# A two-layer graph transformer: raw rows for layer 2's first chunks, batch-norm moments taken block by block, and other places for the table blocks

## The chip, the cores and the metric

The kernel runs on one core of a Trainium2 chip. The metric is the device time of one execution in microseconds. The kernel before takes 2332.54 us (median of three runs, 2331.6 to 2333.5).

## The reference

N = 6250 nodes with 128 features, E = 106250 edges sorted by destination (random pairs in both directions and one loop per node). Every edge has 64 given features and 32 made from a time difference; the two together are its `edge_attr`. Both layers are a transformer convolution with two heads of 64:

```
q, k, v = h@Wq+bq, h@Wk+bk, h@Wv+bv              # by node, 2 heads
e       = edge_attr @ We                          # by edge
alpha   = (q[dst] * (k[src] + e)).sum(c) / 8      # by edge and head
a       = softmax of alpha over the edges of one dst
out     = segment_sum((v[src] + e) * a, dst) + h@Ws + bs
```

and the whole is

```
edge_attr = [cos((node_vec[src] - edge_weight) * time_w + time_b), edge_attr_64]
h = conv1(x)
h = relu((h - mean(h)) / sqrt(var(h) + 1e-5) * bn_g + bn_b)     # over all nodes, by feature
y = layernorm(x + conv2(h))
```

What matters here is the line in the middle: mean and variance are taken over all 6250 nodes, so no row of layer 2's input is known in its final form before the last node of layer 1 is done. Everything is float32.

## The kernel before, in words

**Chunks.** The sorted edge list is cut into NC = 107 chunks of at most CE = 1024 edges (T = 8 tiles of 128) that belong to at most NN = 64 destination nodes. The function `conv(c, extra)` runs one layer as a software pipeline over these chunks. The loop is `for k in range(-AHEAD, NC + 3)` with AHEAD = 4, and one round of it does, in this order, for different chunks:

- `fetch(k + 4)` (L713 to 738): SP loads the chunk's edge features into the tile `ff`, a slice of the table into `ftab`, and in layer 2 also the encoded times (`fz`), the turned edge features (`fxT`) and 64 rows for the residual (`fr`);
- `gather(k + 4)` (L743): GpSimd issues eight indirect DMAs that fetch the source nodes' rows into `ff`, from `xv_d` in layer 1 and from `h_d` in layer 2;
- `score(k)` (L809, L810), `lowest(k)` (L815), `weigh(k)` (L822): scores of all edges against 64 nodes x 2 heads on TensorE, the minimum on VectorE, the exponential on ScalarE;
- `turn_weights(k - 1)` (L832, L833): the weights are transposed;
- `divide(k - 2)`, `finish_turn(k - 2)`, `finish(k - 2)` (L844 to L901): the sums are normalised and multiplied by the value weights; in layer 1 the 64 new rows are written as columns of the tile `hT` by an SP DMA (L870, `fhT<-fres`), in layer 2 they go to the layer norm and to the output;
- `turn_in(k + 1)` (L792, L793): the gathered rows are transposed on TensorE and copied by ScalarE to `fft`;
- `encode(k + 2)` or later (L760 to L774, layer 1): the time encoding; from chunk SINGLE = 24 on, two chunks share one sine on ScalarE, before that each has its own;
- `pull(extra, 1)`: one piece of other work, see below;
- `gather_sums(k - 1)` (L839): the weighted sums, eight matmuls.

The whole loop stands under a manual schedule: each engine's instructions stand in the order in which they are written. The tile `ff` has six buffers, so the gather of chunk k + 4 writes where chunk k - 2 was.

**Tables.** A score needs, for each destination node, four (layer 2) or five (layer 1) numbers per feature. They are made in 13 blocks of 512 nodes by `tables` (L622 to L637): one 128x512 matmul per piece (`fpg`, L627), an eviction by ScalarE (L629, L631) or VectorE (L633) into `fo`, and a store to `tab_d` from ScalarE's queue. `tables` is a generator and yields after each piece; `conv` draws pieces from it through `extra`. In layer 1, six pieces are pulled at the very start of the loop (k = -4), and then one in each round from k = -4 on. In layer 2, blocks 0 and 1 with their residual (L1030 to L1033) are made before the loop, and the rest one piece per round from k = -4 on.

**Between the layers** (L975 to L1014): ScalarE and VectorE sum `hT` (L982, L983), ScalarE sums the squares over all 6250 columns (L988), a few small operations give `scale` and `shift`; then 13 times: ReLU with scale and shift on ScalarE (L1003), four transposes on TensorE (L1006), a copy by VectorE (L1008) and a store of 512 rows to `h_d` by SP (L1011, L1014). Layer 2's first gather waits for the last of these stores, since it can address any row.

Of the kernel before, what the change touches and what calls it, by code (L numbers as in the profile page):

```python
# [621 lines left out]
def tables(nc, pl, c, fT, b0, work, bank):  # L622

    o = work.tile([P, GE, H, 3 - c], F32, name="fo", tag="fo")
    for i, (a, b) in enumerate(pl.mats[c]):
        pg = bank()
        nc.tensor.matmul(pg, a, fT, start=True, stop=True)  # L627
        if i == 2 * H:
            nc.scalar.activation(o[:, :, :, 2], pg[:, :, None].to_broadcast([P, GE, H]), AF.Identity, bias=b)  # L629
        elif i < H:  # L630
            nc.scalar.activation(o[:, :, i, 0], pg, AF.Identity, bias=b)  # L631
        else:
            nc.vector.scalar_tensor_tensor(  # L633
                o[:, :, i - H, 1].rearrange("p (b n) -> p b n", n=P), pg.rearrange("p (b n) -> p b n", n=P), b,
                pl.code[:, None, :].to_broadcast([P, GE // P, P]), op0=OP.add, op1=OP.add)
        if i == len(pl.mats[c]) - 1:
            nc.scalar.dma_start(pl.tab_d[c][:, b0 * GE:(b0 + 1) * GE], o)  # L637
        yield
# [22 lines left out]
def ordered(ctx: ExitStack, tc: tile.TileContext, pl, x, dst, edge_attr_64, conv2, bn_g, bn_b, out):  # L661
# [11 lines left out]
    h_d = dram.tile([N, D], F32, name="h_d")  # L673
    res_d = dram.tile([NP, D], F32, name="res_d")
# [17 lines left out]
    SINGLE = 24  # L692

    def conv(c, extra):
# [45 lines left out]
        def gather(k):  # L740
            f = ch[k].f
            for t in range(T):
                nc.gpsimd.indirect_dma_start(  # L743
                    out=f[:, t, (1 if c else 0):1 + D], out_offset=None, in_=h_d if c else pl.xv_d,
                    in_offset=bass.IndirectOffsetOnAxis(ap=pl.srcs[:, t, k:k + 1], axis=0))
# [37 lines left out]
        def turn_in(k, u):  # L783

            s = ch[k]
            if u == 0:
                s.ft = work.tile([P, CE], F32, name="fft")
                if c == 0:
                    s.et = work.tile([EC, CE], F32, name="fet")
            px = p_tr.tile([P, GE], F32, name="fpx", tag="tr")  # L790
            for t in range(4):
                nc.tensor.transpose(px[:, t * P:(t + 1) * P], s.f[:, u * 4 + t, 1:1 + D], ident)  # L792
            nc.scalar.copy(s.ft[:, u * GE:(u + 1) * GE], px)  # L793
            if c:
                return
            pe = p_tr.tile([P, GE], F32, name="fpe", tag="tr")
            for t in range(4):
                nc.tensor.transpose(pe[:EC, t * P:(t + 1) * P], s.f[:, u * 4 + t, 1 + D:], ident)
            nc.scalar.copy(s.et[:, u * GE:(u + 1) * GE], pe[:EC])  # L799
            if u:  # L800
                nc.sync.dma_start(et_d[k], s.et)
# [39 lines left out]
        def divide(k):  # L841
# [5 lines left out]
            nc.vector.tensor_scalar(s.a, s.pa, inv, None, op0=OP.mult)  # L847

# [62 lines left out]
        with cs, tc.manual_schedule():  # L911
            for k in range(-AHEAD, NC + 3):
# [6 lines left out]
                if k == -AHEAD and c == 0:  # L919
                    pull(extra, 6)  # L920
# [24 lines left out]
                pull(extra, 1)  # L945
# [4 lines left out]
                if c and on(k):  # L950
                    nc.vector.tensor_copy(ch[k].f[:, :, 1 + D:1 + D + TD], ch[k].z)
                for _ in range(min(len(done), 2 if k > NC - 12 else 1)):
                    store(*done.pop(0))
                if on(k - 1):
                    gather_sums(k - 1)
            for _ in extra:
                pass
# [6 lines left out]
    with tc.tile_pool(name="fpw", bufs=2) as pw:  # L964
        with tc.tile_pool(name="ftp", bufs=3, space=bass.MemoryType.PSUM) as mp, tc.manual_schedule():
            turn_features(nc, pl, mp, N)
        def rest():
            for b0 in range(1, NT):
                yield from tables(nc, pl, 0, xT[:, b0 * GE:(b0 + 1) * GE], b0, pw, lambda: pl.bank())
                if b0 == 2:  # L970
                    yield from load_others(nc, pl, const, conv2, bn_g, bn_b)
            yield from matrices(nc, pl, 1, const, lambda: pl.bank()[:, :P])

        conv(0, rest())
    nc.gpsimd.memset(hT[:, N:], 0.0)  # L975


    with tc.tile_pool(name="fbn1", bufs=1) as one, tc.tile_pool(name="fbnw", bufs=2) as pw:
        neg = one.tile([P, 2], F32, name="fmu")
        half = N // 2  # L980
        scr = pl.xT
        nc.vector.tensor_reduce(neg[:, 0:1], hT[:, :half], AX.X, OP.add)  # L982
        nc.scalar.activation(scr[:, half:N], hT[:, half:N], AF.Copy, accum_out=neg[:, 1:])  # L983
        mu = one.tile([P, 1], F32, name="fmu1")
        nc.vector.tensor_add(mu, neg[:, 0:1], neg[:, 1:])
        nc.vector.tensor_scalar(mu, mu, -1.0 / N, None, op0=OP.mult)
        var = one.tile([P, 1], F32, name="fbvar")
        nc.scalar.activation(scr[:, :N], hT[:, :N], AF.Square, bias=mu, accum_out=var)  # L988
        nc.vector.tensor_scalar(var, var, 1.0 / N, EPS, op0=OP.mult, op1=OP.add)
        nc.scalar.activation(var, var, AF.Sqrt)  # L990
        scale = one.tile([P, 1], F32, name="fscale")
        nc.vector.reciprocal(scale, var)
        nc.vector.tensor_mul(scale, scale, pl.bng)
        shift = one.tile([P, 1], F32, name="fshift")
        nc.vector.tensor_mul(shift, scale, mu)
        nc.vector.tensor_add(shift, shift, pl.bnb)
        NB = -(-N // P)
        with tc.tile_pool(name="fbnh", bufs=4) as hp, \
                tc.tile_pool(name="fbnp", bufs=2, space=bass.MemoryType.PSUM) as pps:
            for b0 in range(0, NB, 4):  # L1000
                n = min(4, NB - b0)
                cs_ = slice(b0 * P, b0 * P + GE)
                nc.scalar.activation(hT[:, cs_], hT[:, cs_], AF.Relu, bias=shift, scale=scale)  # L1003
                pt = pps.tile([P, 4, P], F32, name="fpt")
                for i in range(n):
                    nc.tensor.transpose(pt[:, i], hT[:, (b0 + i) * P:(b0 + i + 1) * P], ident)  # L1006
                hr = hp.tile([P, 4, P], F32, name="fhr")
                nc.vector.tensor_copy(hr[:, :n], pt[:, :n])  # L1008
                full = min(n, (N - b0 * P) // P)
                if full:  # L1010
                    nc.sync.dma_start(h_d[b0 * P:(b0 + full) * P, :].rearrange("(b p) d -> p b d", p=P), hr[:, :full])  # L1011
                if full < n:
                    left = N - (b0 + full) * P
                    nc.sync.dma_start(h_d[(b0 + full) * P:N, :], hr[:left, full])  # L1014
# [27 lines left out]
        with tc.tile_pool(name="fpp2", bufs=1, space=bass.MemoryType.PSUM) as pp:  # L1042
            pl.bank = lambda: pp.tile([P, GE], F32, name="fpg")
            for b0 in range(2):
                for _ in block(b0):
                    pass

        def rest():
            for b0 in range(2, NT):
                yield from block(b0)  # L1050

        conv(1, rest())
# [4 lines left out]
def tile_gnn_resnorm(ctx: ExitStack, tc: tile.TileContext, x, src, dst, edge_attr_64, edge_weight, node_vec,  # L1057
# [13 lines left out]
    with tc.tile_pool(name="plan", bufs=1) as pl, tc.tile_pool(name="planw", bufs=2) as mw, \  # L1071
# [7 lines left out]
        got.hT = keep.tile([P, NP], F32, name="fhT")  # L1079
        got.rest = keep.tile([P, 1 + D], F32, name="fxrest")  # L1080
# [27 lines left out]
        ones = pl.tile([P, P], F32, name="pones")  # L1108
# [157 lines left out]
```

## Time and profile before

| what | value |
|---|---|
| time, median of three runs | 2332.54 us |
| the profiled execution | 2840.8 us, span 2838.6 us |
| mean granted TensorE clock in the profile | 0.941 |
| busy: TensorE / VectorE / ScalarE / GpSimd | 84% / 44% / 44% / 58% |
| first layer 1 chunk turned on TensorE | 105.2 us |
| last TensorE work of layer 1 | 1447.2 us |
| first gather of layer 2 | 1480.2 us |
| last gather | 2777.8 us |

The profiled execution is longer than the shown runs by 508 us, so times in the profile are not parts of the 2332 us; a difference between two profiles is not the difference of two runs. The page's fifth part lists groups of instructions: line, engine, operation, output<-input, shape, count | busy us, mean ns | idle time of the engine just before them and what ended it. "issue" there is time in which the engine waited for nothing that the profile shows. In timelines a line is: start us, duration us, engine, line, operation, tiles, count, and in brackets the idle time before it. Some matmuls appear as two records ("x2").

### The profile page before, as it was taken

How to read it: one execution, taken by the hardware profiler on the slowest of the kernel's cores; microseconds unless marked ns; L12 is line 12 of the kernel's file. 1: busy time of each engine (PE TensorE's matmuls, PEld its weight loads, DVE VectorE, ACT ScalarE, POOL GpSimd, SP SyncE). 2: the span in 40 equal slices, each digit the busy share in tenths (PEclk: the TensorE clock that was granted, in tenths of full speed). 3: DMA queues.
4: the chain of work that ended last, by engine and by line, in shares of the span. 5: the costliest groups of instructions: out<-in, count | busy, mean ns of one | idle time of the engine just before them, and what ended most of it. 6: DMA issues, size and time to landing. Idle time of an engine off the chain costs nothing.

```text
span 2838.6 us, 39250 instructions
## 1 busy us (share of the span) xinstructions
PE 2380.1 (84%) x11637; PEld 1759.9 (62%) x11637; DVE 1246.3 (44%) x3735; ACT 1236.5 (44%) x1950; POOL 1637.7 (58%) x1733
## 2 busy tenths in 40 slices
PE   5589988888988888888965989988998888888887
PEld 3366766666776776666742666656666665666665
DVE  3446665555665566565621333333333222222223
ACT  2356664455554455544541333333433333333334
POOL 4356665655665666666415666666666666666661
PEclk7799999999999999999976999999999999999998
DMA  6345554555554445454425555655555454444541
GB/s 198 116 117 155 157 151 144 146 144 166 157 155 127 124 135 137 134 136 136 124 75 165 154 151 155 170 147 156 156 152 151 133 138 127 133 128 131 136 127 46
DMA packets 428354, 396.58 MB, mean 140 GB/s; under 512 B 282064, under 2 KB 371940, under 8 KB 424804
## 3 DMA queue, kind: packets, MB, share of 16 engines
q1 hardware_dynamic: 354406, 238.66, 30.3%
q0 software_dynamic: 55168, 114.12, 15.7%
q10 hardware_dynamic: 18558, 41.20, 3.9%
q8 instruction: 95, 1.56, 0.2%
q14 instruction: 127, 1.04, 0.1%
HBM read 279.72 MB, written 110.59 MB: 138 GB/s over the span
## 4 chain that ended last, share of the span: by engine, by line
PE 34%; issue 6%; another core or an unknown queue 3%; DVE 3%; DMA 2%; POOL 2%; ACT 1%; SPq 1%; DVEq 0%; ACTq 0%; POOLq 0%
PE fpa L839 11%; PE fps L809 6%; PE fps L810 5%; PE fppt L832 4%; PE fpx L792 3%; POOL ff L743 2%; PE fpo L875 1%; PE fpg L627 1%; DMA fr<-res_d 1%; PE fpo L853 1%; DMA ff<-h_d,fsrcs 1%; PE fpo L876 1%; DVE fa L847 1%; PE fpo L854 0%
## 5 line engine op out<-in xcount | busy, mean ns | idle before, releaser
L743 POOL DMA_INDIRECT ff<-xv_d,fsrcs x856 | 822.3, 961 | 568.3 <-issue 224.4
L743 POOL DMA_INDIRECT ff<-h_d,fsrcs x856 | 810.9, 947 | 517.9 <-issue 249.9
L839 PE MATMUL fpa<-ff,fpt 128*128 128x225 f32 x3424 | 714.6, 362 | 0.8 <-issue 0.8
L839 PEld LDWEIGHTS fpa<-ff,fpt 128*128 128x128 f32 x3424 | 645.9, 194 | 14.6 <-issue 0.9
L809 PE MATMUL fps<-fft,ftab 128*128 128x512 f32 x856 | 464.7, 622 | 74.2 <-issue 33.0
L793 ACT COPY fft<-fpx 128x512 f32<-128x512 f32 x428 | 250.2, 585 | 545.7 <-PE fpx L792 202.3
L832 PEld LDWEIGHTS fppt<-fident,fs 128*128 128x128 f32 x1712 | 208.6, 144 | 201.8 <-issue 194.9
L832 PE MATMUL fppt<-fident,fs 128*128 128x128 f32 x1712 | 253.8, 279 | 79.0 <-issue 77.0
L833 ACT COPY fpt<-fppt 128x512 f32<-128x512 f32 x428 | 227.6, 581 | 117.8 <-PE fppt L832 50.0
L822 ACT ACTIVATE fs<-fps,fm 128x1024 f32<-128x1024 f32 x214 | 238.7, 1115 | 66.1 <-issue 27.6
L815 DVE TENSOR_REDUCE flow<-fps 128x1 f32<-128x1024 f32 x214 | 260.0, 1215 | 12.5 <-PE fps L810 12.5
L792 PE MATMUL fpx<-fident,ff 128*128 128x128 f32 x1712 | 254.1, 284 | 12.1 <-DVE fbits L726 12.1
L891 ACT ACTIVATE fsq<-fy 64x128 f32<-64x128 f32 x107 | 33.1, 310 | 503.7 <-DVE fy L889 286.4
L887 DVE SCALAR_TENSOR_TENSOR fres<-fpo,fr 64x128 f32<-64x128 f32 x107 | 30.2, 282 | 501.5 <-PE fppt L832 211.0
L810 PE MATMUL fps<-fxT,ftab 112*128 112x512 f32 x428 | 231.3, 618 | 7.3 <-issue 6.4
L809 PEld LDWEIGHTS fps<-fft,ftab 128*128 128x128 f32 x856 | 171.7, 230 | 104.1 <-issue 56.1
L810 PE MATMUL fps<-fet,ftab 112*128 112x512 f32 x428 | 224.3, 605 | 0.8 <-issue 0.8
L792 PEld LDWEIGHTS fpx<-fident,ff 128*128 128x128 f32 x1712 | 209.8, 147 | 17.1 <-DVE fbits L726 13.7
L799 ACT COPY fet<-fpe 112x512 f32<-112x512 f32 x214 | 126.3, 590 | 198.1 <-PE fppt L832 56.0
L853 PEld LDWEIGHTS fpo<-fident,fa 128*128 128x128 f32 x214 | 30.5, 142 | 286.8 <-issue 184.9
L856 DVE COPY fat<-fpo 128x256 f32<-128x256 f32 x214 | 90.9, 425 | 247.9 <-PE fpo L854 102.5
L853 PE MATMUL fpo<-fident,fa 128*128 128x128 f32 x214 | 64.0, 299 | 157.1 <-DVE fa L847 95.3
(198 smaller groups left out, 2540.7 us busy)
## 6 DMA issues: line engine op xcount, KB each, us to landing
ff<-in_edge_attr SPq DMA_DIRECT2D x214, 256.0 KB
et_d<-fet SPq DMA_DIRECT2D x107, 448.0 KB
fxT<-et_d SPq DMA_DIRECT2D x107, 448.0 KB
ftab<-tab_d SPq DMA_DIRECT2D x107, 192.0 KB
tab_d<-fo ACTq DMA_DIRECT2D x13, 1536.0 KB
ff<-xv_d,fsrcs POOLq DMA_INDIRECT x856
enc_d<-fzs SPq DMA_DIRECT2D x107, 128.0 KB
ff<-h_d,fsrcs POOLq DMA_INDIRECT x856
```

The lines of the kernel that those rows point to most:

```text
L743: nc.gpsimd.indirect_dma_start(out=f[:, t, (1 if c else 0):1 + D], out_offset=None, in_=h_d if c else pl.xv_d, in_offset=bass.IndirectOffs ...
L792: nc.tensor.transpose(px[:, t * P:(t + 1) * P], s.f[:, u * 4 + t, 1:1 + D], ident)
L793: nc.scalar.copy(s.ft[:, u * GE:(u + 1) * GE], px)
L799: nc.scalar.copy(s.et[:, u * GE:(u + 1) * GE], pe[:EC])
L809: nc.tensor.matmul(s.ps[:, w], s.tab[:, :, 0], s.ft[:, w], start=True, stop=False)
L810: nc.tensor.matmul(s.ps[:, w], s.tab[:EC, :, 1], s.et[:, w], start=False, stop=True)
L815: nc.vector.tensor_reduce(low, s.ps, AX.X, OP.min)
L822: nc.scalar.activation(s.s, s.ps, AF.Exp, bias=s.bias, scale=-1.0)
L832: nc.tensor.transpose(pp[:, t * P:(t + 1) * P], s.s[:, at:at + P], ident)
L833: nc.scalar.copy(s.pt[:, u * GE:(u + 1) * GE], pp)
L839: nc.tensor.matmul(s.pa, s.pt[:, t * P:(t + 1) * P], s.f[:, t, 1:1 + D + EW], start=t == 0, stop=t == T - 1)
L853: nc.tensor.transpose(s.po[:, 0], s.a[:, :D], ident)
```

## The change

Five edits. (1) Layer 1's rows are passed on while layer 1 runs: `pass_rows` takes a block of 512 columns of `hT` once all chunks that can write to it are finished, transposes it, stores it unnormalised to `h_d`, and takes its moments with one `bn_stats`; after the loop, one `bn_aggr` joins the 13 moments. (2) Chunks 0 to 2 of layer 2 (RAW = 3) gather from this raw `h_d`. Their rows are normalised when needed: in `turn_in` by ScalarE, whose copy becomes a ReLU with scale and shift (features are partitions there), and in `normalise` by three VectorE operations for the sums. (3) All later chunks gather from a new tensor `hn_d`, which `first_blocks` writes at round k = -4 of layer 2: ReLU of the blocks, transposes, copies, and stores from ScalarE's queue instead of SP's. (4) Table blocks move: no piece is pulled before round 0; two per round are pulled in rounds 0 to 3 and after round 80; two empty steps follow each block; in layer 2 only block 0 is made ahead, through three PSUM banks instead of one. `fo` has one buffer instead of two. (5) SINGLE is 16 instead of 24. The diff has nothing else on the sine or its buffers.

```diff
-    o = work.tile([P, GE, H, 3 - c], F32, name="fo", tag="fo")
+    o = work.tile([P, GE, H, 3 - c], F32, name="fo", tag="fo", bufs=1)
...
-    SINGLE = 24
+    SINGLE = 16
+    RAW = 3
...
-                    out=f[:, t, (1 if c else 0):1 + D], out_offset=None, in_=h_d if c else pl.xv_d,
+                    out=f[:, t, (1 if c else 0):1 + D], out_offset=None, in_=(h_d if k < RAW else hn_d) if c else pl.xv_d,
...
-            nc.scalar.copy(s.ft[:, u * GE:(u + 1) * GE], px)
+            if c and k < RAW:
+                nc.scalar.activation(s.ft[:, u * GE:(u + 1) * GE], px, AF.Relu, bias=pl.shift, scale=pl.scale)
+            else:
+                nc.scalar.copy(s.ft[:, u * GE:(u + 1) * GE], px)
...
+        def normalise(k):
+            rows = ch[k].f[:, :, 1:1 + D]
+            for i, op in enumerate((OP.mult, OP.add)):
+                nc.vector.tensor_tensor(rows, rows, pl.spread[:, None, i].to_broadcast([P, T, D]), op)
+            nc.vector.tensor_scalar(rows, rows, 0.0, None, op0=OP.max)
...
-                if k == -AHEAD and c == 0:
-                    pull(extra, 6)
+                if k == -AHEAD and c:
+                    first_blocks()
...
-                pull(extra, 1)
+                if k >= 0:
+                    at_round[0] = k
+                    pull(extra, 2 if k < 4 or k > 80 else 1)
...
                 if c and on(k):
+                    if k < RAW:
+                        normalise(k)
...
+        def pass_rows(b0):
+            r0 = b0 * GE
+            n = min(GE, N - r0)
+            rows = turned_rows(b0)
+            nc.vector.bn_stats(stats[:, b0], hT[:, r0:r0 + n])
+            yield
+            put_rows(nc.sync, h_d, b0, rows)
+            yield
+        def turned_rows(b0):
+            r0 = b0 * GE
+            n = -(-min(GE, N - r0) // P)
+            pt = pl.bank().rearrange("p (b d) -> p b d", d=P)
+            for i in range(n):
+                nc.tensor.transpose(pt[:, i], hT[:, r0 + i * P:r0 + (i + 1) * P], ident)
+            rows = pw.tile([P, GE // P, P], F32, name="fhr", bufs=3)
+            nc.vector.tensor_copy(rows[:, :n], pt[:, :n])
+            return rows
...
         def rest():
+            others = load_others(nc, pl, const, conv2, bn_g, bn_b)
             for b0 in range(1, NT):
                 yield from tables(nc, pl, 0, xT[:, b0 * GE:(b0 + 1) * GE], b0, pw, lambda: pl.bank())
-                if b0 == 2:
-                    yield from load_others(nc, pl, const, conv2, bn_g, bn_b)
+                for _ in range(2):
+                    next(others, None)
+                    yield
             yield from matrices(nc, pl, 1, const, lambda: pl.bank()[:, :P])
+            for b0 in range(-(-N // GE)):
+                while at_round[0] < 3 + max(k for k in range(NC) if first(k)[0] < (b0 + 1) * GE):
+                    yield
+                yield from pass_rows(b0)
...
-        nc.vector.tensor_reduce(neg[:, 0:1], hT[:, :half], AX.X, OP.add)
-        nc.scalar.activation(scr[:, half:N], hT[:, half:N], AF.Copy, accum_out=neg[:, 1:])
...
-        nc.scalar.activation(scr[:, :N], hT[:, :N], AF.Square, bias=mu, accum_out=var)
...
+        nc.vector.bn_aggr(moments, stats)
...
-            for b0 in range(0, NB, 4):
-                n = min(4, NB - b0)
...
-                nc.scalar.activation(hT[:, cs_], hT[:, cs_], AF.Relu, bias=shift, scale=scale)
...
-                    nc.sync.dma_start(h_d[b0 * P:(b0 + full) * P, :].rearrange("(b p) d -> p b d", p=P), hr[:, :full])
...
+        def first_blocks():
+            for b0 in range(1, NT):
+                relu(b0)
+            for b0 in range(-(-N // GE)):
+                put_rows(nc.scalar, hn_d, b0, turned_rows(b0))
-        with tc.tile_pool(name="fpp2", bufs=1, space=bass.MemoryType.PSUM) as pp:
+        with tc.tile_pool(name="fpp2", bufs=3, space=bass.MemoryType.PSUM) as pp, tc.manual_schedule():
             pl.bank = lambda: pp.tile([P, GE], F32, name="fpg")
-            for b0 in range(2):
-                for _ in block(b0):
-                    pass
+            relu(0)
+            for _ in block(0):
+                pass
...
+            for i, col in enumerate((scale, shift)):
+                nc.vector.tensor_scalar(diag[:, i], ident, col, None, op0=OP.mult)
+                nc.tensor.matmul(pb[:, i], pl.ones, diag[:, i], start=True, stop=True)
+            nc.vector.tensor_copy(spread, pb)
         def rest():
-            for b0 in range(2, NT):
+            for b0 in range(1, NT):
                 yield from block(b0)
-        conv(1, rest())
+                yield
+                yield
+        conv(1, rest(), first_blocks)
```

`put_rows(eng, to, b0, rows)` is the store of one block of rows, as at L1011 and L1014, from the given engine's queue.

## The prediction

> **What bounds the kernel now.** I read the page's busy table first, then the chain of waits in the middle of a layer, then the engines' timelines around the two places where TensorE stands still: the fill of layer 1 and the turn from layer 1 to layer 2. The page:
>
> ```profile
> span 2838.6 us, 39250 instructions
> PE 2380.1 (84%) x11637; PEld 1759.9 (62%) x11637; DVE 1246.3 (44%) x3735; ACT 1236.5 (44%) x1950; POOL 1637.7 (58%) x1733
> L743 POOL DMA_INDIRECT ff<-h_d,fsrcs x856 | 810.9, 947 | 517.9 <-issue 249.9
> ```
>
> TensorE is the busiest engine; GpSimd looks half idle but its 856 gathers per layer each end in a fixed gap. The chain shows an undisturbed chunk of layer 1, when no gather runs any more (columns: start us, us, what):
>
> ```profile
> 1403.01 0.92 PE fps L809 x2
> 1403.94 0.86 PE fps L810 x2
> 1405.02 0.44 PE fpx L792 x4
> ...
> 1407.21 3.04 PE fpa L839 x16
> ...
> 1412.85 0.92 PE fps L809 x2
> ```
>
> From score to score 1403.01 to 1412.85 is 9.84 us of TensorE at full clock with nothing between. In layer 2 the same chain has fpa starts at 1932.46 and 1942.60: 10.14 us with one table piece (fpg, 0.87 us) in it, so 9.27 without. GpSimd in a run of gathers:
>
> ```profile
> 1481.46 0.95 POOL L743 DMA_INDIRECT ff<-h_d,fsrcs  x1 [0.30 <-issue]
> 1482.71 0.94 POOL L743 DMA_INDIRECT ff<-h_d,fsrcs  x1 [0.30 <-issue]
> ```
>
> One gather every 1.25 us, 8 per chunk: 10.0 us. So both engines need about 10 us per chunk, and they overlap. What overlaps with nothing is the fill and the turn. The turn on TensorE and in the chain:
>
> ```profile
> 1446.77 0.39 PE L864 MATMUL fpo<-fat,fwe 128*128 128x128 f32 x2
> 1461.93 5.58 PE L1006 MATMUL fpt<-fident,fhT 128*128 128x128 f32 x24 [14.77 <-ACT fhT L1003]
> 1475.31 2.08 PE L627 MATMUL fpg<-fhT,fm 128*128 128x512 f32 x2 [1.99 <-DVE fhr L1008]
> 1512.09 1.04 PE L792 MATMUL fpx<-fident,ff 128*128 128x128 f32 x8
> 1532.36 2.08 PE L809 MATMUL fps<-fft,ftab 128*128 128x512 f32 x2 [14.40 <-issue]
> ```
>
> ```profile
> 1469.90 4.29 DMA h_d<-fhr
> 1475.48 3.35 DMA h_d<-fhr
> ```
>
> Layer 1 ends at 1447.2. Moments over the whole of hT take until 1461 (ACT L983 2.9, L988 5.6, a table load 1.28); normalising, turning and storing h_d until 1478.9; GpSimd starts gathering at 1480.2; meanwhile TensorE makes table blocks 0 and 1, one piece per 3.3 us through a single PSUM bank, until 1507.4, and three pieces of block 2, before chunk 0 is turned at 1512.1. Then all engines stall ("issue") until 1532.
>
> The profiled execution took 2840.8 us, the runs 2332.5. I read the difference as stalls that the shown runs mostly lack: TensorE's floor is 107 x 9.84 + 107 x 9.27 + 102 table pieces in the loops x 0.87 = 2134 us, which leaves 199 us for everything else, while the profile shows 105 (to the first chunk, 105.17) + 85 (1447.2 to 1532.4) + some 33 (drains and end) = 223. Without the stalls I estimate head 66, turn 67, drains and end 33, that is 166. The last 33 us fit a per-chunk floor by GpSimd of about 9.8 us under the 56 chunks of layer 2 that carry no table piece (56 x 0.53 = 30), or a granted clock 1.5% under full.
>
> **What the Trainium skill says.** "TensorE: Matmul & The Clock Gate", Part 1: the array runs at half clock after an idle window of about 3.4 us. The trace agrees: table pieces in the turn take 2.08 us per pair of records, 1.02 in the loop. "DMA: Bandwidth & Descriptors", Anatomy of one DMA (told there for GpSimd's path): about 2 us fixed, most of it the write's receipt. Here SP's 256 KB stores take 4.29 and 3.35, and these are used. "VectorE: DVE Perf Modes", TRN2 errata: a float32 tensor_tensor takes (N+151)/0.96 ns; the trace agrees (fxr, 512 elements, 0.69). So each normalising product of 1024 elements is an estimated 1.22 us.
>
> **The change, part by part.**
>
> *The turn.* After the last fhT lands (1449.5): one transpose 0.3, copy 0.3, bn_stats and bn_aggr (not in the trace; each between the 0.15 of the smallest DVE operation and the 0.7 of a 128x512 copy, I take 0.3), five small DVE operations at 0.16 and the Sqrt 0.2, whose table load waits for nothing: scale and shift at about 1453 = s, not 1461. The last h_d store goes at 1450.3 and lands 3.4 later, so raw gathers start near 1455 (25 us earlier) and the three raw chunks are issued by 1485. Block 0 now has three banks: four pieces at 2.08, ACT and DVE evictions behind them, residual: s+13. The order puts ScalarE's last four ReLUs (0.71 each) behind block 0's stores: hn_d stores start at s+16. fhr has three buffers, so copy n waits for store n-3 to land: store 12 leaves at s+20.3+4L, and the last lands at s+20.3+5L, with L the landing time. With L = 4: stores end at s+36.3 and s+40.3. TensorE holds 49 transposes for hn_d ahead of chunk 0's, ScalarE 13 store issues ahead of its copy: chunk 0 is scored at about s+38 = 1491. Before, without the stall, it is 1514 (1513.1 + a copy). Gain 23 us. Gather 3 waits for all 13 stores, 1493; GpSimd idles 8 us there with all later gathers behind it. Chunk 3's rows land at 1505 and TensorE wants them two rounds after 1491, at 1513: hidden, with 8 us to spare.
>
> *Layer 1.* 9 table pieces leave the fill and join the loop: 9 x 0.87 = +7.8. 49 transposes (0.11 each at full clock) for the raw rows: +5.4. Their DVE copies (13 x 0.69) and bn_stats, and 13 stores on SP, hide beside a DVE that is 60% busy; SP's fhT store and next fetch stand behind each store, which waits only for a 0.7 copy. The transposes read columns whose fhT stores left a round earlier and land in 1.8: no wait. Sum +13.
>
> *Layer 2's loop.* Block 1 and four pieces of block 2 also join: 9 x 0.87 = +7.8 on TensorE if that is the bound. But pieces now come 5 in 7 rounds over 84 rounds and not in each of the first 51. A round averages 9.27 + 0.62 = 9.89, where before 51 took 10.14 and 56 took GpSimd's 9.8. With that floor: before 51 x 10.14 + 56 x 9.8 = 1066; after 84 x 9.89 + 23 x 9.8 = 1056, -10 if buffers smooth fully. I take -3, between +7.8 and -10.
>
> *The fill of layer 1.* Nine pieces no longer stand before chunk 0. Its gathers are issued by 54 and land at 56; in an undisturbed run the pieces delay its encoding to some 62: gain 5. In the profile first chunk work is at 105, so up to 25 if stalls are real. I take 5.
>
> *At nothing.* SINGLE 16: four sines fewer and up to eight table loads fewer at 1.28, on a ScalarE under 70% busy; 0 to -5 where a score waits for it. Normalising three chunks: 2 x 1.22 and one max of 0.6 to 1.2, about 3.5 us of DVE per round, under gather_sums' 3.2 us of TensorE and a DVE that is 30% busy in layer 2; uncovered it would be 3 x 3.5. One fo buffer: the next block's first eviction comes 1.5 rounds after the store in the first four rounds, three later; a late one would hold ScalarE, 0 to 5 once. ReLU in the copy costs as the copy.
>
> Sum: -23 + 13 - 3 - 5 = -18. The profiled time would go from 2840.8 to about 2823, or lower by 25 more where its stalls at 1516 to 1543 vanish; the runs from 2332.5 to 2314.
>
> **Rivals.** A: TensorE alone is the bound; then layer 2 pays +7.8: -23 + 13 + 7.8 - 5 = -7, 2325. For it, 84% busy and the dense chain; against it, GpSimd's 10.0 us. B: the stalls under gather bursts are real in the shown runs too: the turn gains 1532.4 - 1491 = 41, the fill 25: -41 + 13 - 3 - 25 = -56, 2277, probably half of it, 2290. For it, they stand in the trace; against it, the 199 us budget. C, slower: the three fhr buffers. Each store's landing counts four times before chunk 0. If L is not 4 but near 10 us (three raw gathers, the edge rows and 448 KB of fxT share the DMA engines then), 23 of gain becomes 0 and the moved work is left: 4 x (L - 4) = 23 decides for no gain on the turn, and the sum is +0.2% from L = 9.7 on. At L = 11 the sum is -18 + 28 = +10, 2342. Against it: with gathers running, tab_d's 1 MB store issued at 1488.5 let SP go on at 1492.8, 4.3 us. D: the moved work and the shorter turn cancel, 2332.
>
> **How the numbers follow.** The forecast 0.42, A 0.22, B 0.16, C 0.13, D 0.07. The range runs from B's half, 2285, to C's near end, 2338. No change of under 0.2% (4.7 us) can be told from none by this measurement. Faster: forecast, A and B, 0.80; same D, 0.07; slower C, 0.13.
>
> **What would show it.** Of the changed kernel's profile: last layer 1 work to the first score 45 us, not 85 (to 97); the first h_d gather some 8 us after that work and hn_d's first about 45 after; a wait of POOL for hn_d under 15 us; DVE's fhr copies waiting for hn_d stores, some 16 us in all; TensorE unbroken in rounds 84 to 93 of layer 1. Wrong if the fhr copies wait over 40 us, if chunk 3 waits for its gather, or if layer 1's loop grows by over 20.

## The result and the profile after

The changed kernel takes 2324.49 us (median of 13 runs, 2321.6 to 2329.3); the kernel before, run beside it, 2331.52 (13 runs). The ratio is 0.9972 with a 95% interval of 0.9963 to 0.9981: 7 us faster, 0.28%. In a second group of runs the ratio was 0.9966 (0.9954 to 0.9978). The forecast was 2314, 18 us faster: the sign is right, the size is not.

The profiled execution of before that the prediction worked from took 2840.8 us, and in two groups of runs below the kernel before took some 2853 and 2886 us, the other kernels there as much longer, where it takes 2332 to 2337 elsewhere. So the two kernels are compared here by a second profile of before, whose execution took 2334 us; the profiled execution of the changed kernel took 2324.5 and agrees with its runs.

The page of the changed kernel: span, busy times, the gathers of normalised rows, and the transposes of gathered rows:

```profile
span 2322.7 us, 39390 instructions
PE 2230.6 (96%) x11690; PEld 1724.1 (74%) x11690; DVE 1248.9 (54%) x3771; ACT 1202.9 (52%) x1934; POOL 1643.7 (71%) x1733
L748 POOL DMA_INDIRECT ff<-hn_d,fsrcs x832 | 790.3, 950 | 265.6 <-issue 221.3
L797 PE MATMUL fpx<-fident,ff 128*128 128x128 f32 x1712 | 249.6, 276 | 22.1 <-DMA ff<-hn_d,fsrcs 12.7
```

TensorE is busy 96% of the span, and still the transposes of layer 2 wait 12.7 us for gathered rows (11.7 in the second profile of before): GpSimd, busy 71%, is late somewhere. The timelines of TensorE and GpSimd around the turn, kernel before (second profile):

```profile
1187.65 0.39 PE L864 MATMUL fpo<-fat,fwe 128*128 128x128 f32 x2
1255.25 1.02 PE L809 MATMUL fps<-fft,ftab 128*128 128x512 f32 x2
1221.04 0.95 POOL L743 DMA_INDIRECT ff<-h_d,fsrcs  x1 [30.09 <-issue]
2291.92 0.95 POOL L743 DMA_INDIRECT ff<-h_d,fsrcs  x1 [0.30 <-issue]
```

and of the changed kernel:

```profile
1191.64 0.39 PE L878 MATMUL fpo<-fat,fwe 128*128 128x128 f32 x2
1236.44 2.08 PE L817 MATMUL fps<-fft,ftab 128*128 128x512 f32 x2 [1.90 <-ACT fft L799]
1198.91 0.94 POOL L748 DMA_INDIRECT ff<-h_d,fsrcs  x1 [50.89 <-ACT fhT L1074]
1240.86 0.94 POOL L748 DMA_INDIRECT ff<-hn_d,fsrcs  x1 [12.30 <-DMA fr<-res_d]
2283.48 0.94 POOL L748 DMA_INDIRECT ff<-hn_d,fsrcs  x1 [0.30 <-issue]
```

In each: layer 1's last matmul, layer 2's first score, layer 2's first gather, (after) the first gather of normalised rows, the last gather of all. The profile ends the 12.30 us before the first normalised gather with a load of `fr`, the last to land by the profile; by the program this gather waits for the stores of `hn_d`, whose last one is issued at 1234.95, and two experiments below shorten the wait by acting on these stores or by doing without them. Two ledgers follow, each of which sums to the 9.1 us between the two spans.

By TensorE's milestones:

| stretch | before | after | measured | forecast |
|---|---|---|---|---|
| start to first score | 64.3 | 57.5 | -6.8 | -5 |
| first score to layer 1's end | 1123.7 | 1134.5 | +10.8 | +13 |
| layer 1's end to first score of layer 2 | 67.2 | 44.4 | -22.8 | -23 |
| from there to the end of the span | 1076.6 | 1086.3 | **+9.7** | **-3** |

By GpSimd's:

| stretch | before | after | measured |
|---|---|---|---|
| start to layer 1's end | 1188.0 | 1192.0 | +4.0 |
| layer 1's end to first gather | 33.0 | 6.9 | -26.1 |
| first to last gather, without the wait | 1070.9 | 1072.6 | +1.7 |
| wait ahead of the fourth chunk, over the usual 0.3 | 0 | 12.0 | +12.0 |
| last gather to the end | 39.9 | 39.2 | -0.7 |

These are single profiles. In a profile of another kernel with before's layer 1, that layer ends at 1184.1, and in five more of kernels with the change's layer 1 between 1191.0 and 1196.2, so rows that contain layer 1 are good to some 4 us only. The rows of the turn hold better: first gather after 32.9 us there, and 6.8 to 7.0.

In the first table one row is far off its forecast. The second says why: 856 gathers take 1071 and 1073 us, which is 1.25 each, the bare cadence. Layer 2 lasts as long as GpSimd needs for its gathers, and the new wait stands in that row of gathers undiminished. The busy times by window (columns: window, its length; then busy us and count of TensorE, weight loads, VectorE, ScalarE and GpSimd; granted clock, DMA share, GB/s), before and then after:

```profile
1500.00:1600.00 100.00, 100.00 (x525) 73.50 (x524) 40.19 (x129) 45.70 (x87) 75.80 (x80) 1.00 0.71 187
2000.00:2100.00 100.00, 96.09 (x507) 71.86 (x506) 34.53 (x126) 41.52 (x84) 75.62 (x81) 1.00 0.61 161
```

```profile
1500.00:1600.00 100.00, 100.00 (x533) 74.20 (x531) 41.00 (x132) 43.94 (x86) 75.62 (x81) 1.00 0.71 186
2000.00:2100.00 100.00, 96.64 (x523) 73.51 (x522) 37.29 (x130) 43.70 (x88) 75.62 (x81) 1.00 0.66 172
```

GpSimd issues 80 or 81 gathers per 100 us in every one of these windows: busy 76%, and yet without a pause, since each gather of 0.95 us is followed by 0.30 in which it issues nothing. TensorE is full in the 1500s, while it has table pieces to do and works on chunks that were gathered ahead. This lead, from the end of a chunk's last gather to its first transpose, is 20.2 us before and 3.6 us after at chunk 48; at chunk 88 it is 1.1 and 1.6 us. In both kernels it is used up before the end, and TensorE, idle 3 to 4% of the 2000s, waits for gathers. A share of 71% on the page was an engine at its limit.

### The profile page after: what moved, and what is told of

The parts are those of the page before. It is cut to its first block, busy times and chain, and to the rows that moved or that the text cites. A ratio compares the mean times of both kernels' runs of the same rounds, so it can differ in the third digit from the quotient of the medians.

```text
span 2322.7 us, 39390 instructions
## 1 busy us (share of the span) xinstructions
PE 2230.6 (96%) x11690; PEld 1724.1 (74%) x11690; DVE 1248.9 (54%) x3771; ACT 1202.9 (52%) x1934; POOL 1643.7 (71%) x1733
## 3 DMA queue, kind: packets, MB, share of 16 engines
q0 software_dynamic: 55168, 114.12, 20.3%
q14 instruction: 127, 1.04, 0.1%
## 5 line engine op out<-in xcount | busy, mean ns | idle before, releaser
L748 POOL DMA_INDIRECT ff<-hn_d,fsrcs x832 | 790.3, 950 | 265.6 <-issue 221.3
L847 PE MATMUL fpa<-ff,fpt 128*128 128x225 f32 x3424 | 701.2, 357 | 0.0
L817 PE MATMUL fps<-fft,ftab 128*128 128x512 f32 x856 | 447.8, 605 | 3.6 <-ACT fft L799 1.9
L797 PE MATMUL fpx<-fident,ff 128*128 128x128 f32 x1712 | 249.6, 276 | 22.1 <-DMA ff<-hn_d,fsrcs 12.7
L840 PE MATMUL fppt<-fident,fs 128*128 128x128 f32 x1712 | 222.2, 272 | 0.0
L818 PE MATMUL fps<-fxT,ftab 112*128 112x512 f32 x428 | 220.0, 595 | 0.0
L818 PEld LDWEIGHTS fps<-fet,ftab 112*128 112x128 f32 x428 | 107.5, 251 | 76.7 <-issue 58.9
L818 PEld LDWEIGHTS fps<-fxT,ftab 112*128 112x128 f32 x428 | 84.8, 198 | 100.8 <-issue 100.1
L772 DVE SCALAR_TENSOR_TENSOR farg<-fturns,farg 128x256 f32<-128x256 f32 x321 | 136.8, 426 | 11.0
L852 DVE TENSOR_SCALAR finv<-fpa 128x1 f32<-128x1 f32 x214 | 32.7, 153 | 197.9 <-issue 93.1
L806 PE MATMUL fpe<-fident,ff 128*112 128x128 f32 x856 | 130.0, 275 | 1.4 <-DVE ff L784 1.4
```

The source lines that it names most:

```text
L748: nc.gpsimd.indirect_dma_start(out=f[:, t, (1 if c else 0):1 + D], out_offset=None, in_=(h_d if k < RAW else hn_d) if c else pl.xv_d, in_o ...
L772: nc.vector.scalar_tensor_tensor(arg, turn, -part, arg, op0=OP.mult, op1=OP.add)
L817: nc.tensor.matmul(s.ps[:, w], s.tab[:, :, 0], s.ft[:, w], start=True, stop=False)
L818: nc.tensor.matmul(s.ps[:, w], s.tab[:EC, :, 1], s.et[:, w], start=False, stop=True)
L840: nc.tensor.transpose(pp[:, t * P:(t + 1) * P], s.s[:, at:at + P], ident)
L847: nc.tensor.matmul(s.pa, s.pt[:, t * P:(t + 1) * P], s.f[:, t, 1:1 + D + EW], start=t == 0, stop=t == T - 1)
```

## The experiments

**Theories.** Theory 1: layer 2 goes at GpSimd's pace, ten microseconds a chunk from its first gather on; what counts at the turn is when GpSimd starts and for how long it must pause, not when TensorE scores the first chunk. Theory 2 (rival A of the prediction): TensorE is the bound throughout; layer 2 pays 7.8 us for the table pieces that joined its loop. Theory 3: the turn of before was shorter, undisturbed, than the forecast took it.

Medians are compared with the kernel before on the same chip; the change itself has 0.9972 and 0.9966.

| kernel | median us | before beside it | ratio (95%) |
|---|---|---|---|
| one more raw chunk | 2319.43 | 2337.14 | 0.9930 (0.9917 to 0.9943) |
| eight buffers for normalised rows | 2320.74 | 2337.14 | 0.9929 (0.9916 to 0.9941) |
| seven gathers a chunk | 2303.21 | 2337.14 | 0.9857 (0.9840 to 0.9874) |
| the change again | 2326.69 | 2334.18 | 0.9966 (0.9954 to 0.9978) |
| before, with three PSUM banks at the turn | 2333.39 | 2334.18 | 0.9994 (0.9986 to 1.0003) |
| fill of layer 1 as before | 2314.39 | 2334.18 | 0.9914 (0.9901 to 0.9926) |
| one more raw chunk and eight buffers | 2315.90 | 2334.18 | 0.9923 (0.9911 to 0.9935) |
| two steps a round from 85 on | 2317.98 | 2331.68 | 0.9943 (0.9931 to 0.9956) |
| one more raw chunk and the fill as before | 2306.48 | 2331.68 | 0.9896 (0.9881 to 0.9910) |
| the same, sine switch at 24 | 2300.13 | 2331.68 | 0.9866 (0.9852 to 0.9880) |

**The kernel before, profiled again**

> The kernel before once more, for a profile whose execution is as long as its runs (the one shown took 2840.8 us). Theory 1 (layer 2 goes at GpSimd's pace, ten microseconds a chunk from its first gather on): the first gather of layer 2 starts about 33 us after layer 1's last work, GpSimd gathers without a pause of more than 1 us from there, and the time from that gather to the end is about 1110 us, as in the kernel after. Theory 2 (TensorE alone is the bound): the first score of layer 2 comes within 60 us of layer 1's last work, GpSimd waits for buffers in most rounds of layer 2, and TensorE is busy over 99% of it. Theory 3 (the undisturbed turn was shorter than the forecast took it): the first score comes less than 75 us after layer 1's last work.

Its lines are shown above. First gather 33.0 us after layer 1's end, and 1110.8 us from there to the end of the span, as theory 1 says, and no gather between waits longer than the usual 0.3. What theory 2 asked for isn't there: the first score comes after 67.2 us, not within 60, and TensorE is busy 96% in the 2000s. Theory 3 allows 67.2 too, but 67 is what the prediction had estimated for the undisturbed turn. So theory 3 is out: the turn's size was no surprise.

**Does TensorE's first score count?** The kernel before, one edit: the table blocks made at the turn get three banks.

```diff
-        with tc.tile_pool(name="fpp2", bufs=1, space=bass.MemoryType.PSUM) as pp:
+        with tc.tile_pool(name="fpp2", bufs=3, space=bass.MemoryType.PSUM) as pp:
```

> The kernel before with one edit: the table blocks of its turn use three PSUM banks in place of one, so that TensorE doesn't wait 1.25 us for an eviction at each of some eight pieces; the gathers stay where they were. Theory 1 (layer 2 goes at GpSimd's pace from its first gather on): the first score of layer 2 comes 8 to 10 us earlier (57 to 59 us after layer 1's last work, not 67), and the time doesn't move by more than 3 us. Theory 2 (TensorE's turn is what counts): the time falls by 8 to 10 us.

From its timelines: layer 1's last matmul, layer 2's first score, its first gather.

```profile
1183.67 0.39 PE L864 MATMUL fpo<-fat,fwe 128*128 128x128 f32 x2
1233.55 1.58 PE L809 MATMUL fps<-fft,ftab 128*128 128x512 f32 x2
1216.96 0.95 POOL L743 DMA_INDIRECT ff<-h_d,fsrcs  x1 [29.99 <-DVE fo L633]
```

The first score comes 49.5 us after layer 1's end in place of 67.2, a gain of 17.7, more than expected; the first gather stays at 32.9. The time is that of before, 0.9994. From the first score to the end of the span it is 1096.1 us, 19.5 more than in the kernel before: what TensorE gains at the turn it loses again later. Nearly 18 us of TensorE's turn are worth 1.4, at most some 3. This alone refutes the step in which the prediction put TensorE's 23 us into its sum, and theory 2 with it.

**Does GpSimd's wait count?** The change with four raw chunks.

```diff
-    RAW = 3
+    RAW = 4
```

> One more raw chunk, so that gather 3 needn't wait for the normalised rows. Theory 1: GpSimd's wait of 12.3 us ahead of the fourth chunk's gathers falls to under 3 us (the wait moves to chunk 4 and is covered by eight gathers), and the time falls by 8 to 12 us, to about 2314. Theory 2: GpSimd's start is worth nothing, TensorE has the same work, VectorE one normalise more (3.2 us, hidden): within 2 us of the change.

The gathers around the switch to normalised rows, in this kernel:

```profile
1240.15 0.94 POOL L748 DMA_INDIRECT ff<-h_d,fsrcs  x1 [0.30 <-DMA hn_d<-fhr]
1243.12 0.94 POOL L748 DMA_INDIRECT ff<-hn_d,fsrcs  x1 [0.78 <-DMA fxT<-et_d]
```

The wait is gone (0.78), and so are 0.4% of the time, some 9 us, although TensorE has the same work and VectorE more. From the first score to the end of the span it is 1076.8 us (1238.44 to 2315.2), 9.5 less than in the change and 0.2 from the kernel before's 1076.6, although layer 2's loop carries the added table pieces. So the +9.7 of the first ledger is the wait, and not the pieces: rival A's +7.8 for them doesn't show.

**The stores that GpSimd waits for.** Five more buffers out of columns of `xT` that layer 2 first writes at its chunk 4.

```diff
-                put_rows(nc.scalar, hn_d, b0, turned_rows(b0))
+                i = b0 % 8 - 3
+                spare = xT[:, 4 * CE + i * GE:4 * CE + (i + 1) * GE].rearrange("p (b d) -> p b d", d=P) if i >= 0 else None
+                put_rows(nc.scalar, hn_d, b0, turned_rows(b0, spare))
```

> The normalised rows go out from eight buffers in place of three (five of them columns of xT that layer 2 first writes at its chunk 4), so that VectorE's copies don't wait for the stores' landings. Theory 1: the 16 us that VectorE waits there fall to under 5, the last store lands 8 to 12 us earlier, GpSimd's wait of 12.3 us falls to 1 to 5 us, and the time falls by 7 to 10 us, to about 2316. Theory 2: the first score comes 8 to 12 us earlier on TensorE, and the time falls by about as much. A third view (landings are set by the queue's bandwidth beside the gathers and loads): the landings stretch to 10 us or more each, and the last comes no more than 4 us earlier.

First the chain of the changed kernel in the turn (start us, us, what), then the busy row of the same stretch (the DMA share books a transfer whole where it starts and so can pass 1); below them such a row and the first normalised gather with eight buffers.

```profile
1211.09 6.54 DMA hn_d<-fhr
1218.47 6.78 DMA hn_d<-fhr
1226.10 6.45 DMA hn_d<-fhr
```

```profile
1220.00:1235.00 15.00, 5.34 (x21) 3.51 (x20) 4.39 (x11) 0.00 (x0) 6.60 (x7) 0.50 1.05 292
```

```profile
1225.00:1238.00 13.00, 3.94 (x5) 1.85 (x6) 0.00 (x0) 1.45 (x2) 6.01 (x7) 0.50 1.10 324
1238.09 0.95 POOL L748 DMA_INDIRECT ff<-hn_d,fsrcs  x1 [5.25 <-DMA fxT<-et_d]
```

A landing on this chain takes 6.5 us or more in the change, not the 4 of the forecast. With eight buffers VectorE's waits for stores fall from 16.4 us to some 2, but GpSimd still pauses 5.25; the gain is 0.4%, 9 us. The DMA engines are full in both windows (share over 1, 292 and 324 GB/s), so I take them, not buffers, as what is left; no run tests it. The Trainium skill, "DMA: Bandwidth & Descriptors", Bandwidth, gives a core some 358 GB/s when both cores that share an HBM domain stream, and 425 measured for one alone; these windows stay below both figures, so the rate alone doesn't show a limit. Theory 1's sizes held, the pause by a hair not (1 to 5 us). Of the third view the crowded DMA engines held, its figures did not: landings on the chain are some 6 us, and the last store is issued 6.4 us earlier, counted from scale and shift.

> Four raw chunks and the eight buffers for the normalised rows together. Theory 1: with either alone GpSimd's wait is 5 us or none, so together they give what four raw chunks give alone, within 3 us: some 10 us below the change. Theory 2: TensorE's first score comes earlier by the stores' 16 us of waits less what covers them, and the two add up: 15 us or more below the change.

Both together: 0.9923, the same as either alone (0.9930, 0.9929). The first score comes 36.3 us after layer 1's end, 8 earlier than in the change, and brings nothing that these intervals show once GpSimd doesn't wait. Theory 1.

**How far is TensorE's own bound?** GpSimd relieved of one gather in eight.

```diff
             for t in range(T):
+                if c and k >= RAW and t == T - 1:
+                    nc.sync.dma_start(f[:, t, 1:1 + D], hn_d[:P, :])
+                    continue
                 nc.gpsimd.indirect_dma_start(
```

> From layer 2's fourth chunk on, the last of a chunk's eight gathers is replaced by a plain load of 128 rows issued by SyncE (so these edges get wrong source rows: that part of the computation is left out). It frees GpSimd of 1.25 us in every chunk and leaves TensorE's work as it was. Theory 1: layer 2 leaves GpSimd's pace and becomes TensorE's; TensorE's idle time of layer 2 after its first rounds (about 15 us) goes, and the time falls by 10 to 20 us, to about 2310. Theory 2: TensorE was the bound all along; the time stays within 4 us of the change.

From the first score to the last matmul, busy times in the change and then here:

```profile
1236.44:2311.48 1075.04, 1056.39 (x5534) 780.70 (x5534) 417.52 (x1361) 474.52 (x916) 790.29 (x832) 1.00 0.65 171
```

```profile
1235.24:2290.50 1055.26, 1049.59 (x5534) 779.99 (x5534) 415.93 (x1361) 474.42 (x916) 690.28 (x728) 1.00 0.65 174
```

TensorE's gaps in layer 2 go from 18.7 to 5.7 us and the kernel is 26 us faster than the change (21 by the spans of the two profiles), beyond what theory 1 expected (10 to 20): TensorE's busy time for the same 5534 instructions falls by 7 as well. Theory 2 gave it 4. GpSimd's pause of 11.7 us at the turn is still there in this kernel and does no harm, because here GpSimd has slack to catch up.

**The fill of layer 1.** The change, with its table pieces where the kernel before has them at the start.

```diff
+                if k == -AHEAD and c == 0:
+                    pull(extra, 6)
...
-                if k >= 0:
-                    at_round[0] = k
-                    pull(extra, 2 if k < 4 or k > 80 else 1)
+                at_round[0] = k
+                if k >= 0 or c == 0:
+                    pull(extra, 2 if k > 80 or c and k < 4 else 1)
```

> The changed kernel with its fill of layer 1 as before: six table pieces pulled at the first step of the fill and one at each further step, and one a round from then on. The prediction priced the edit at -5 (fill) and +7.8 (nine pieces that join TensorE's loop), so undoing it should take 2.8 us off. Layer 1: its first score comes 5 to 7 us later, and from that score to layer 1's last work it takes 6 to 8 us less. Layer 2 is untouched. Both theories: within 3 us of the change, more likely below it. A third view (the nine pieces are hidden in the loop): 4 to 7 us slower.

No expectation held: it is 12 us faster than the change in the same group (0.9914 against 0.9966). In the change (its second group of runs): VectorE's first operation on the second, third and fourth gathered chunk, then on TensorE layer 1's first score, a wait, and the first weighted sums:

```profile
60.11 0.17 DVE L765 TENSOR_TENSOR frel<-ff,few 128x8 f32<-128x8 f32 x1 [3.90 <-DMA ff<-xv_d,fsrcs]
70.14 0.17 DVE L765 TENSOR_TENSOR frel<-ff,few 128x8 f32<-128x8 f32 x1 [4.12 <-DMA ff<-xv_d,fsrcs]
80.16 0.17 DVE L765 TENSOR_TENSOR frel<-ff,few 128x8 f32<-128x8 f32 x1 [2.89 <-DMA ff<-xv_d,fsrcs]
58.87 1.86 PE L817 MATMUL fps<-fft,ftab 128*128 128x512 f32 x2
76.61 0.66 PE L797 MATMUL fpx<-fident,ff 128*128 128x128 f32 x4 [3.37 <-ACT fo L631]
82.30 3.20 PE L847 MATMUL fpa<-ff,fpt 128*128 128x225 f32 x16
```

and with the old fill (first score, third chunk on VectorE, first weighted sums):

```profile
63.71 1.02 PE L817 MATMUL fps<-fft,ftab 128*128 128x512 f32 x2
70.14 0.17 DVE L765 TENSOR_TENSOR frel<-ff,few 128x8 f32<-128x8 f32 x1 [1.38 <-DMA ff<-xv_d,fsrcs]
78.56 3.20 PE L847 MATMUL fpa<-ff,fpt 128*128 128x225 f32 x16
```

VectorE starts on a new chunk every 10 us, at GpSimd's pace again, in the change each time after a wait for its rows, and on the third at 70.1 in both. So the fill, too, goes by gathers. The change scores at 58.9 in place of 63.7 and then runs into the same gathers: its first weighted sums start at 82.3, those of the old fill at 78.6. The pieces it moved out of the fill had been free there; now their evictions stand on ScalarE behind a sine that waits for a gather, and TensorE waits 3.4 us for them. The first weighted sums come 3.7 us later. The loop holds five more rounds with a piece (54 rounds of 10.69 us against 49; without one a round takes 9.84), 4.3 us. The rest is the next experiment.

**Two long rounds.** In the change, rounds 80 and 81 of layer 1 take 14.7 and 13.8 us where their neighbours take 10.3. From its timeline of TensorE:

```profile
936.61 0.48 PE L595 MATMUL fpg<-ftr,ftr 64*128 64x128 f32 x2 [2.50 <-ACT fft L801]
951.21 0.48 PE L595 MATMUL fpg<-ftr,ftr 64*128 64x128 f32 x2 [1.18 <-ACT fft L801]
```

Two weight-matrix pieces fall into one round there, because the moved table pieces push the matrices past round 80, where two steps a round begin. The two waits are 3.7 us of the 8 that these rounds are too long; over the 5 us from 935 on the granted clock is 0.78, over the next 5 it is 0.88, and 1.00 before. The test:

```diff
-                    pull(extra, 2 if k < 4 or k > 80 else 1)
+                    pull(extra, 2 if k < 4 or k > 84 else 1)
```

> The changed kernel with one number changed: two steps a round from round 85 on, not from 81. In the profile of the change the two rounds after 80 are 14.7 and 13.8 us long, because two weight-matrix pieces stand in one round and the second waits for ScalarE's eviction of the first (2.5 and 1.2 us), after which TensorE's clock drops. If that is the cost, layer 1 ends 6 to 8 us earlier and the time falls by as much; if the rounds are long for another reason (gathers, the stores of h_d), it stays within 2 us of the change or the long rounds move to 85.

Beside a kernel before of 2853 us it gave 0.990 (0.987 to 0.994), and in another group, beside one of 2886 us, 0.983 (0.977 to 0.989). The change itself wasn't run in these groups, and the intervals are wider than the effect. Beside a kernel before of 2332 us:

> Two steps a round from round 85 on, a third time, for a comparison where the kernel before takes some 2333 us. If two weight-matrix pieces in one round are the cost of the long rounds after 80: layer 1 ends 6 to 8 us earlier than in the change, the time is 0.6% to 0.7% below the kernel before. If not: 0.3% below, as the change.

0.9943 against 0.9972 and 0.9966: 5 to 7 us. The rounds with matrix pieces are 10.56, 10.56 and 12.6 us now (one pair is left), and the loop from the first to the last weighted sums is 5.0 us shorter (1101.0 against 1106.0). So the collision is a real third part of the 12: 3.7, 4.3 and 5.0 make 13, measured 12.

**The sine switch, and whether the costs add.** The change with the old switch, and a kernel with two edits undone:

> The changed kernel with the number of rounds that each turn one chunk's sine set back from 16 to 24. The prediction priced this edit at nothing to -5; undoing it would then cost 0 to 5 us. Against it: in the profile of the change the rounds at 15 and 16, where VectorE encodes two chunks, are 3.2 and 4.2 us over their neighbours, in the kernel before the round at 23 is 2.4 over. If the place of the switch matters, layer 1 is 3 to 5 us shorter with 24, and the time falls so.

> Four raw chunks, and the fill of layer 1 as in the kernel before. Theory 1 (the wait of GpSimd and the nine table pieces are separate costs in series): their gains add, 10 for the first and 12 for the second, so 20 to 24 us below the change, 1.2 to 1.3% below the kernel before. Theory 2 (both earlier gains came from one thing, or TensorE caps layer 2): 12 to 15 us below the change.

Beside the kernel before of 2853 us they gave 0.988 and 0.987; beside the one of 2886 us, 0.978 and 0.981, and 0.968 for both edits with the switch at 24 as well. The intervals are 0.5% to 1% to each side: nothing to tell them apart by. The switch at 24 was not run alone beside a kernel before of some 2332 us; there it is read from the difference of these two:

> Four raw chunks with the fill of before, a third time, for the same reason. Theory 1: the gains add, 1.2% to 1.3% below the kernel before (2302 to 2306 where that takes 2333). Theory 2: 0.85% to 1.0% below, as the better of the two alone.

> The same with the sine switch at 24, for the same reason. If the place of the switch is what makes rounds 15 and 16 long: 3 to 5 us below the one with 16. If it is worth nothing or a gain: 0 to 5 us above it.

Four raw chunks with the old fill give 0.9896, some 17 us below the change; the parts gave 9 and 12. That is 1.04% below before, with an interval of 0.90% to 1.19%: it misses the 1.2% that addition asked for and reaches into theory 2's 0.85% to 1.0%, so the runs don't show that the two gains add in full. The profile speaks for two separate costs: on top of the old fill GpSimd's wait falls by 9.0 us (10.8 to 1.8), and its time from first to last gather by 6.9. The other 2.1 us are in the gathers themselves, which took that much longer in sum; why is open.

With the sine switch at 24 it is 2300.13 us, 0.9866: some 31 us below the kernel before and 24 below the change. The edit that the prediction put at nothing to -5 therefore costs 6 by the medians (four runs each), 2 by the spans (2305.0, 2302.8). The rounds at the switch are 17.3 us (at 15) in one and 14.4 (at 23) in the other, with neighbours of 10.7: VectorE encodes two chunks in that round, and TensorE waits for its division, 5.0 us in the early round and 1.9 in the late one. That makes 2.9 of it; the rest, and why the early wait is longer, is not accounted for.

## Why the prediction was right and wrong

**The turn, -23: right in size (-22.8), wrong in use.** Raw gathers 6.9 us after layer 1's end (some 8 forecast), 16.4 us of VectorE waiting for stores (16), first score at 44.4 (45). Part of this is luck, since inside it two errors cancelled: from the first store of `hn_d` to the last 24.4 us passed and not 20.3, as landings were longer than 4, and the stores began 12.8 us after scale and shift, not 16. But the banks' experiment shows that this number is not a term of the total.

**Layer 2's loop, -3: the step that failed; it measured +9.7.** The prediction had the fact in hand ("one gather every 1.25 us, 8 per chunk: 10.0 us"), and mixed it into an average of TensorE rounds (10.14, 9.89, 9.8). It then took 8 us of GpSimd's pause as costing nothing, and TensorE's 23 us as a gain. With 10.0 as the floor of all 107 chunks, the time runs from GpSimd's first gather: it starts 26 us earlier, pauses 12, layer 1 ends 4 later, and what is left is -9 in the spans and -7 in the runs. The sentence that hid the pause, "hidden, with 8 us to spare", was true of chunk 3 and false of the engine: the gathers of chunk 3 and all 103 after it stood behind the wait, and TensorE first waited for one of them at 1799 us, 560 us later.

**GpSimd's pause, 8: mis-sized, 12.3** (10.8 to 12.3 in the profiles with this turn), since the stores took longer; the first normalised gather comes 48.8 us after layer 1's end, not 45. It is under the 15 that the prediction set as its mark, and that mark was too lenient: nearly all of it counts (ending it gave some 9 us).

**The fill, -5: measured -6.8 at the first score, and nothing at the first weighted sums** (80.8 before, 79.9 after). In other profiles with these fills the first score comes at 61.3, and at 58.0 to 59.7, the first weighted sums at 79.1, and at 79.9 to 83.2: so -5 may be right for the one, and the other is no gain. The same mistake in small: the gathers' pace was not applied to the fill.

**Layer 1, +13: measured +10.8** from first score to end (9 to 14 over all pairs of profiles), by other parts than forecast. Pieces and transposes are there (rounds of 10.69 and 10.27); added are 5.0 for the collision and some 2 to 4 at the sine switch, which the prediction missed; against that, twelve microseconds of waits for VectorE's divisions spread over the kernel before's layer 1 (13 waits) shrink to four in the change (3 waits), nearly all of them at the switch. What removes the others was not tested.

**SINGLE, 0 to -5: wrong sign,** +2 to +6. **Normalising, hidden: right;** its three operations take 1.23, 1.23 and 0.69 us, as estimated, and a fourth chunk of it cost nothing that shows. **The ReLU in the copy** doesn't cost as the copy: 0.78 us against 0.58, six times, and nothing shows of it.

**Rival A** named 2325 and got the number by luck, from a cause that the runs refute: freeing GpSimd or ending its wait pays, freeing TensorE's turn doesn't. Rival B's stalls are not in the second profile of before (its turn takes 67.2 us, not 85); and what it calls half is not half, since half of its 56 us would give 2304 and not 2290. Rival C's mechanism was real, at two thirds of the landing time that it needed (6.5 of 9.7). D, no gain, lies outside the interval.

The signs that the prediction listed for itself came, or nearly: first score, first gather and first normalised gather 44.4, 6.9 and 48.8 us after layer 1's end, a pause of GpSimd under 15 us, copies that wait 16.4 us, no gap on TensorE in rounds 84 to 93. None of the three listed for "wrong" occurred: copies waited 16 us, not 40; chunk 3 didn't wait; layer 1 didn't grow by 20. And the time was still wrong: no sign looked at what the turn's gain was worth at the end of layer 2.

## What to carry to other kernels

Look for an engine that issues at a fixed cadence without a pause, whatever its busy share (here 76%), and price a change on that engine's timeline first: its first issue, its pauses, its count times its cadence. An earlier start of TensorE was worth nothing here until that engine was early too, and a wait of 12 us put into its row cost some 9, although the next consumer had slack and the loss showed hundreds of microseconds later. When pieces of other work are moved off a stretch, ask what bounds that stretch: under gathers that arrive every 10 us they were free, and where they went they took time and collided.

## What the runs showed of the hardware

**Gathers.** In layer 2 GpSimd issues a gather of 128 rows every 1.25 us, 0.95 us of work and 0.30 between two, 856 in both kernels. A busy share of 76% was all that it gave.

**Stores.** A store of 256 KB landed after 4.29 and 3.35 us in the turn of before, and after 6.45 to 6.78 us on the chain of the changed kernel's turn, where the DMA share is over 1.

**The first profile.** In the 2840.8 us of the first profile GpSimd pauses some 2.3 us once a chunk in addition, 102 times in layer 2, which makes 12.1 us a chunk and not 10.0. TensorE stops there some 80 times for 0.8 us or more, mostly one to three, with no cause that the profile shows. The second profile of before has no such pause of GpSimd in layer 2. What the pauses are remains open. The prediction read the difference of 20% as stalls that the shown runs mostly lack, and kept them as rival B.
